# Attention taken two blocks of keys at a time: scores, values of two blocks, scores, then projection pieces

## The chip, the cores and the metric

The kernel runs on one core of one Trainium2 chip. The metric is device time in microseconds (us) of one execution, as the median of several. Engines that matter here are TensorE (PE in the profile, its weight loads PEld), VectorE (DVE), ScalarE (ACT), GpSimd (POOL) and SyncE (SP), which issues most DMAs. Each executes its own instruction stream in program order, and semaphores tie the streams together.

## What is computed

The input is 32 batches of 512 tokens by 512 features in float32, and a 512 x 512 adjacency matrix of zeros and ones. Two layers follow each other:

```
# layer 0
mi = x @ Wi.T ; mj = x @ Wj.T ; deg = adj.sum(1)
x  = layernorm(x + deg[:, None] * (mi + b) + adj @ mj)
# layer 1: 8 heads of 64
q, k, v = x @ Wq.T + bq, x @ Wk.T + bk, x @ Wv.T + bv
scores  = where(adj == 0, -inf, (q @ k.T) / 8)
x = layernorm(x + softmax(scores) @ v @ Wo.T + bo)
```

Everything is float32. The attention needs, per batch, 8 heads of 512 x 512 scores.

## The kernel before, in words

**Projections.** Each 512 x 512 product is made by a Strassen-like scheme of seven `piece` calls (line 420), numbered 1 to 7, on 256 x 256 quarters. One piece of kind `pj` (output projection), `v`, `q` or `k` is 8 matmul instructions with 256 moving columns; a piece of layer 0 (`l0`) has two terms and 16. A piece accumulates into a PSUM bank, and a reader then takes the bank's contents into SBUF: VectorE mostly (lines 454, 465, 474, 481), ScalarE for pieces 1 and 2 (lines 443, 463, 479). Pieces are grouped (line 408): 1 and 2 share a bank's contents, so do 6, 7 and 4, and 5 and 3. A later piece of a group adds on top of the earlier one, so its matmuls may start only once the reader of the earlier piece is done. There are two such banks, "mma" and "mmb" (line 86, one buffer each), and the kinds alternate between them. Between pieces stand `l0_gather` (line 316, matmuls with the adjacency matrix, read out by ScalarE at line 340), `l0_turn` (VectorE transpose, line 348, then a multiplication on GpSimd), `base` (two VectorE operations, line 354), `combos` (GpSimd, line 405: differences and sums of quarters), `stats` and `apply` (layer norm: VectorE lines 298 and 299, GpSimd 300 to 302, ScalarE 305), and `h_store`, `h_load`, `h_turn` (the layer-0 result goes to DRAM and comes back regrouped, and VectorE turns it, line 382).

**Attention.** A batch's attention has 8 steps (`STEPS`, line 549): two groups `g` of four heads, and four blocks `kc` of 128 keys for each. In a step, `scores(b, hp, kc)` (line 486) is called for two pairs of heads. It takes a PSUM tile "sc" (two buffers, line 93), makes 4 matmul instructions with 64 rows each, two at a time in the array, then ScalarE takes the exponential in place (line 494), and VectorE multiplies by the 0/1 edge matrix into an SBUF tile "e" (four buffers, lines 492 and 495). `values` (line 505) multiplies the "e" tiles of one block by V: 16 matmul instructions with 32 columns each, four at a time in the array. `presum` (line 497) adds up "e" tiles for the softmax denominators: on GpSimd for block 1 (line 501), on VectorE for blocks 2 and 3 (line 503). After a group's last block, `sums` (line 515) makes the denominators in another "sc" tile, `drain` (line 524) copies them, and `rest` (line 542) lists four reciprocals (`invert`, line 531), two multiplications (`scale`, line 540) and a reduction (`tell`, line 533).

**The order of the work** is written out by hand. `phase_a`, `phase_b` and `phase_c` (lines 567, 622, 644) list a batch's projection work, `by_steps` (line 686) cuts the list into 8 steps by estimated cost, and the loop from line 768 on emits each step. A step is: scores of this block for both pairs, values of the block before, then the pieces of that step. After each item with a cost, at most one waiting `presum` (the list `late`) and some of `rest` (the list `extra`) are emitted. While batch b attends, the loop projects batch b + 1 and finishes batch b - 1; the listing of the middle of the program for `PERIODS[n]` is, for steps 6 and 7: gather 0, k piece 5, turn 0, gather 1, k piece 3, turn 1, base 0, combos, gather 2, k piece 6, turn 2, base 1, gather 3, k piece 7, turn 3, combos, layer-0 piece 1, k piece 4. For steps 4 and 5 it begins with k piece 2, q piece 5, v piece 5, q piece 3, v piece 3.

Of the kernel before, what the change touches and what calls it, by code (L numbers as in the profile page):

```python
# [17 lines left out]
P = 128  # L18
# [7 lines left out]
def gnn_attention_kernel(  # L26
# [37 lines left out]
    B, N, D = x.shape  # L64
    NC = N // P
# [14 lines left out]
    def work(shape, name, bufs, dtype=FT):  # L80
        return pools.work.tile(shape, dtype, name=name, bufs=bufs)
# [7 lines left out]
    def ov_tile():  # L89
        return psum.tile([P, 512], FT, name="ov", bufs=2)  # L90

    def sc_tile():
        return psum.tile([P, 2, N], FT, name="sc", bufs=2)
# [147 lines left out]
    def ring_tile():  # L241
        return work([P, 2, Q], "ring", RING)
# [40 lines left out]
    def prefetch():  # L283
        while len(TILES) < min(len(KEYS), ring.used + RING) and KEYS[len(TILES)] in WS:
            t = ring_tile()
            nc.sync.dma_start(t, WS[KEYS[len(TILES)]])
            TILES.append(t)
# [105 lines left out]
    def ot_quarter(b):  # L393
        return lambda j, n: OT[b, j][:, :, Q * n:Q * n + Q]
# [86 lines left out]
                    nc.vector.scalar_tensor_tensor(d[:, c], pm[:, c, :], bc, p1[:, c, :], op0=OP.add, op1=OP.add)  # L481


    E, ES, PV, RL = {}, {}, {}, {}

    def scores(b, hp, kc):
        ps = sc_tile()
        for s in range(2):
            r = slice(s * HD, (s + 1) * HD)
            nc.tensor.matmul(ps[:, s, :], KT[b, hp // 2][r, hp % 2, kc * P:(kc + 1) * P],  # L490
                             QT[b, hp // 2][r, hp % 2, :], start=True, stop=True)
        e = E[hp % 2, kc] = work([P, 2, N], "e", 4)

        nc.scalar.activation(ps, ps, AF.Exp, scale=QSCALE)  # L494
        nc.vector.tensor_tensor(e, ps, edge[:, kc:kc + 1, :].to_broadcast([P, 2, N]), op=OP.mult)  # L495

    def presum(i, kc):
# [7 lines left out]
    def values(b, g, kc):  # L505

        if kc == 0:
            PV[g] = [ov_tile(), ov_tile()]
        for r in range(2):
            for h in range(4):  # L510
                c0 = (4 * g + h) * HD + 32 * r
                nc.tensor.matmul(PV[g][r][32 * h:32 * h + 32, :], V[b][:, kc, c0:c0 + 32], E[h // 2, kc][:, h % 2, :],  # L512
                                 start=(kc == 0), stop=(kc == NC - 1))

    def sums(g, kcs=(1,), last=1):

        if g not in RL:
            RL[g] = (sc_tile()[:, 0, :], work([P, N], "rl", 1))
        for kc in kcs:
            for h in range(4):  # L520
                src = ES[h // 2] if kc == 1 else E[h // 2, kc]
                nc.tensor.matmul(RL[g][0][32 * h:32 * h + 32, :], ones[:, :32], src[:, h % 2, :], start=(kc == 1), stop=(kc == last))  # L522

    def drain(b, g):

        j = 2 * (b * 2 + g)
        nc.scalar.activation(RL[g][1], RL[g][0], AF.Identity, accum_out=told[:, j:j + 1])
# [14 lines left out]
    def rest(b, g):  # L542
        return [(invert, g, c) for c in range(4)] + [(scale, b, g, 0), (scale, b, g, 1), (tell, b, g)]
# [5 lines left out]
    STEPS = 2 * HP  # L549
    PC, TR, GA = 1.73, 0.44, 1.9  # L550
    FLUSH = (0.0, None)

    def z(f, *a):
        return (0.0, f, *a)

    def pc(kind, b, i, bank):
        return (2 * PC if kind == "l0" else PC, piece, kind, b, i, bank)
# [5 lines left out]
    def banks(n):  # L563

        return ("a", "b") if n % 2 == 0 else ("b", "a")
# [21 lines left out]
    def first():  # L587


        g = [(TR + GA, l0_gather, 0, dc, "b") for dc in range(DC)]  # L590
        half = lambda name, i: z(combine, name, nc.gpsimd if name in ("wi", "wj") else nc.vector, i)
        y = [(8 * PC / 4, plain, ic) for ic in range(NC)]
        n = [(TR, l0_norm, 0, ic) for ic in range(NC)]
        return [g[0], z(graph_forms, 3), g[1], g[2], half("wv", 0), g[3], z(base, 0, 0), z(base, 0, 1), half("wv", 1),
                y[0], z(scaled, 0), half("wq", 0), half("wi", 0), y[1], z(scaled, 1), half("wq", 1), half("wi", 1), z(fold, 0), y[2], half("wk", 0), half("wj", 0),
                z(scaled, 2), n[0], y[3], half("wk", 1), half("wj", 1), n[1], (2 * PC, fold, 1), z(scaled, 3)]
# [16 lines left out]
    def project(m, i):  # L613

        res = [pc("pj", m, i, banks(m)[1])]
        if i == 1:
            res = [z(combos, TO, m, ot_quarter(m), (1,))] + res
        if i == 2:
            res = [FLUSH] + res + [z(combos, TO, m, ot_quarter(m), (2, 3, 4))]
        return res  # L620

    def phase_b(n):

        m = n - 2
        if m < 0:
            res = []
            side = [z(add_bo, 0, i) for i in range(2)]
            A, K = banks(n)
            for i, bank in ((2, A), (6, K), (5, A), (7, K), (4, K), (3, A)):
                res.append(pc("l0", n, i, bank))  # L630
                if i == 4:
                    res += [z(stats, n, 0)]
                if i in (2, 6):
                    res += [z(combine, "wo", nc.vector, int(i == 6))]
                res += side[:1]
                side = side[1:]
            return res + [z(apply, n, 0), z(stats, n, 1), (TR, l0_norm, n, 0), (TR, l0_norm, n, 1)]
        A = banks(n)[0]
        l0 = {i: pc("l0", n, i, A) for i in ORDER}
        return [l0[2], *project(m, 1), l0[6], *project(m, 2), l0[7], z(add_bo, n - 1, 0), *project(m, 6), l0[4], z(stats, n, 0),  # L640
                *project(m, 7), z(apply, n, 0), z(h_store, n, 0), l0[5], z(h_load, n, 0), z(add_bo, n - 1, 1), *project(m, 4),
                l0[3], z(stats, n, 1), z(h_turn, n, 0), *project(m, 5)]

    def phase_c(n):

# [53 lines left out]
    def last_steps():  # L699

        m = B - 2
        A, K = banks(B)
        p = {i: pc("pj", m, i, K if i in (6, 7, 4) else A) for i in ORDER}
        c = [z(combos, TO, m, ot_quarter(m), (1, 2)), z(combos, TO, m, ot_quarter(m), (3, 4))]
        own = [(4 * GA, last_part, c, 0) for c in range(2)]
        k = [pc("k", B - 1, i, K) for i in (7, 4)]
        return [[z(last_load), k[0], FLUSH, c[0], p[1], c[1], k[1]], [p[2], p[6]], [p[5], p[7], z(add_bo, B - 1, 0), z(add_bo, B - 1, 1)],
                [], [p[3], p[4]], [own[0], z(stats, m, 0), z(stats, m, 1)], [own[1], z(apply, m, 0), z(apply, m, 1), z(store, m)], []]

    def run(f):  # L710
        f[1](*f[2:])
# [36 lines left out]
    PERIODS = [first() + phase_c(0) + phase_a(1)]  # L748
    half = None
    for n in range(1, B):  # L750
        todo = phase_b(n) + phase_c(n) + phase_a(n + 1)
# [12 lines left out]
    for f in PERIODS[0]:  # L764
        run(f)
        if f[1] is combine:
            prefetch()
    for n in range(1, B + 1):
        b = n - 1
        extra = []  # L770
        for step in range(STEPS):
            g, kc = divmod(step, NC)
            scores(b, 2 * g, kc)
            scores(b, 2 * g + 1, kc)
            pb, pg, pk = (b, *divmod(step - 1, NC)) if step > 0 else (b - 1, 1, NC - 1)
            if pb >= 0:
                values(pb, pg, pk)
                if pk == NC - 1:
                    sums(pg, *(((1, 3), 3) if pb == B - 1 else ()))
                    drain(pb, pg)  # L780
                    extra = rest(pb, pg)
            late = [(presum, i, kc) for i in range(2) if kc > 0]
            if b == B - 1 and kc > 2 - g:

                late = []
            for f in PERIODS[n][step]:
                if f is FLUSH:
                    some = len(extra)
                else:
                    run(f)  # L790

                    some = 0 if f[0] == 0.0 else len(extra) if step == 0 else max(1, round(f[0] / PC))
                if some:
                    for g in late[:1] + extra[:some]:
                        g[0](*g[1:])
                    late, extra = late[1:], extra[some:]
            for g in late + extra:
                g[0](*g[1:])
            extra = []
    sums(1, (1, 2), 3)  # L800
    values(B - 1, 1, 3)
    sums(1, (3,), 3)
# [1 line left out]
    for ic in range(NC):  # L804
        c = slice(ic * P, (ic + 1) * P)
# [15 lines left out]
    with tc.If(flag > 0), tc.tile_pool(name="general", bufs=1) as pools.work:  # L821
# [30 lines left out]
        with tc.For_i(0, B, 1) as b:  # L852
            g = "general"
# [6 lines left out]
            for ic in range(NC):  # L860
                c = slice(ic * P, (ic + 1) * P)
# [10 lines left out]
            for ic in range(NC):  # L872
                c = slice(ic * P, (ic + 1) * P)
                nc.vector.tensor_copy(V[g][:, ic, :], product([(HT[g][:, dc, c], wv[:, dc, :]) for dc in range(DC)]))
            for hp in range(HP):
                c = slice(hp * P, (hp + 1) * P)
# [5 lines left out]
                for qb in range(NC):  # L882
                    ps = sc_tile()
# [28 lines left out]
            for ic in range(NC):  # L912
                c = slice(ic * P, (ic + 1) * P)
# [45 lines left out]
```

## Time and profile before

| what | value |
|---|---|
| median of 3 executions | 3689.72 us (3689.59 to 3689.89) |
| the profiled execution: its own time | 3689.89 us |
| its span | 3687.9 us |
| TensorE busy | 3662.2 us, 99% of the span |
| VectorE busy | 2393.1 us, 65% |
| GpSimd busy | 1939.0 us, 53% |
| ScalarE busy | 1029.4 us, 28% |
| DMA | 144 GB/s in the mean |

The span runs from the first to the last instruction in the profile; the execution's own time is 1.99 us more. Matmul ends are modelled in this profile and overlap, so the start times of neighbouring matmuls are the better measure of what each costs. Each engine's idle time is put down to what released it. Idle time of an engine that is not the bottleneck costs nothing.

### The profile page before, as it was taken

The numbers are of one execution on the slowest core, as the hardware profiler recorded it, in microseconds if no ns is written. First come the engines' busy times: TensorE is split into PE (matmuls) and PEld (weight loads), VectorE is DVE, ScalarE is ACT, GpSimd is POOL, SyncE is SP. The second block draws the span as 40 slices with busy tenths as digits, with TensorE's granted clock in tenths as the row PEclk, the third lists the DMA queues.
The fourth block names the chain that finished last, engine by engine and source line by source line (L and its number), as shares of the span: only waits on it lengthen the run. The fifth ranks groups of instructions, "written<-read, shape, count | busy, mean of one in ns | idle before, by whom it ended". The sixth has DMA issues, their size and how long they took to land.

```text
span 3687.9 us, 49638 instructions
## 1 busy us (share of the span) xinstructions
PE 3662.2 (99%) x18470; PEld 2511.0 (68%) x18470; DVE 2393.1 (65%) x3133; ACT 1029.4 (28%) x1485; POOL 1939.0 (53%) x1984
## 2 busy tenths in 40 slices
PE   9999999999999999999999999999999999999998
PEld 6766667666666666766666767666666676666663
DVE  4666666666666666666666666666666666666666
ACT  2232232222322223222223222232222322222322
POOL 3565545556455555455554555644555545555443
PEclk9999999999999999999999999999999999999999
DMA  8445455445555445554545544455544555455541
GB/s 257 141 120 143 137 155 160 135 133 138 149 160 148 132 132 149 151 163 122 140 138 154 160 138 131 137 149 159 149 131 132 148 152 161 125 140 138 154 135 50
DMA packets 797173, 530.02 MB, mean 144 GB/s; under 512 B 530432, under 2 KB 611840, under 8 KB 796928
## 3 DMA queue, kind: packets, MB, share of 16 engines
q1 hardware_dynamic: 780384, 494.78, 48.8%
q10 hardware_dynamic: 16320, 31.46, 2.3%
q8 instruction: 151, 2.47, 0.3%
q14 instruction: 94, 0.77, 0.1%
q0 software_dynamic: 224, 0.53, 0.0%
HBM read 453.25 MB, written 73.40 MB: 143 GB/s over the span
## 4 chain that ended last, share of the span: by engine, by line
PE 98%; DVE 1%; POOL 1%; ACT 0%; issue 0%; DMA 0%; SPq 0%; DVEq 0%; POOLq 0%; ACTq 0%
PE mma L436 31%; PE mmb L436 31%; PE sc L490 13%; PE ov L512 13%; PE mmb L334 4%; PE mma L334 3%; PE sc L522 2%; PE mmb L604 0%; PE mma L604 0%; POOL es L501 0%; DVE e L495 0%; DVE rl L531 0%; PE sc L730 0%; DMA big<-in_adj_dram 0%; POOL big L405 0%
## 5 line engine op out<-in xcount | busy, mean ns | idle before, releaser
L494 ACT ACTIVATE sc<-sc 128x1024 f32<-128x1024 f32 x512 | 493.1, 1007 | 1552.9 <-PE sc L490 1534.4
L495 DVE TENSOR_TENSOR e<-sc,edge 128x1024 f32<-128x1024 f32 x512 | 602.6, 1217 | 211.8 <-ACT sc L494 176.7
L436 PE MATMUL mmb<-ring,big 128*128 128x256 f32 x3144 | 731.5, 381 | 0.0
L436 PE MATMUL mma<-ring,big 128*128 128x256 f32 x3112 | 724.4, 381 | 1.5 <-DVE xh L454 0.8
L436 PEld LDWEIGHTS mmb<-ring,big 128*128 128x128 f32 x3144 | 592.1, 190 | 130.0 <-issue 26.8
L436 PEld LDWEIGHTS mma<-ring,big 128*128 128x128 f32 x3112 | 585.9, 190 | 132.3 <-issue 26.5
L490 PE MATMUL sc<-q,k 64*128 64x512 f32 x2048 | 510.5, 617 | 3.5 <-DVE e L495 3.5
L405 POOL TENSOR_TENSOR big<-big 128x512 f32<-128x512 f32 x376 | 492.2, 1336 | 27.0 <-ACT big L363 10.7
L512 PE MATMUL ov<-e,v 128*32 128x512 f32 x4096 | 492.6, 598 | 3.3 <-DVE oT L540 3.3
L501 POOL TENSOR_TENSOR es<-e 128x1024 f32<-128x1024 f32 x128 | 300.1, 2355 | 363.5 <-DVE e L495 363.5
L436 PE MATMUL mma<-big,ring 128*128 128x256 f32 x1808 | 430.5, 381 | 0.0
L436 PE MATMUL mmb<-big,ring 128*128 128x256 f32 x1776 | 422.8, 381 | 0.0
L300 POOL TENSOR_SCALAR mv<-mv 128x1 f32<-128x1 f32 x256 | 49.7, 194 | 664.6 <-DVE mv L299 652.2
L436 PEld LDWEIGHTS mma<-big,ring 128*128 128x128 f32 x1808 | 340.3, 190 | 74.6 <-issue 26.8
L436 PEld LDWEIGHTS mmb<-big,ring 128*128 128x128 f32 x1776 | 334.3, 190 | 72.9 <-issue 26.0
L512 PEld LDWEIGHTS ov<-e,v 128*32 128x32 f32 x4096 | 107.0, 109 | 351.5 <-issue 322.1
L204 POOL TENSOR_TENSOR xlo<-xh,xhi 128x512 fp32r<-128x512 f32 x128 | 162.6, 1281 | 338.7 <-ACT xhi L203 338.6
L490 PEld LDWEIGHTS sc<-q,k 64*128 64x128 f32 x2048 | 176.4, 186 | 211.3 <-issue 203.6
L349 POOL TENSOR_TENSOR big<-big,deg_r 128x512 f32<-128x512 f32 x124 | 173.2, 1397 | 263.7 <-DVE big L348 263.7
L503 DVE TENSOR_TENSOR es<-es,e 128x1024 f32<-128x1024 f32 x250 | 304.2, 1218 | 0.0
L454 DVE TENSOR_TENSOR xh<-xh,mma 128x512 f32<-128x512 f32 x186 | 126.7, 681 | 267.2 <-PE mma L436 267.2
L454 DVE TENSOR_TENSOR xh<-xh,mmb 128x512 f32<-128x512 f32 x186 | 126.7, 681 | 259.4 <-PE mmb L436 259.4
(157 smaller groups left out, 3658.8 us busy)
## 6 DMA issues: line engine op xcount, KB each, us to landing
ring<-wo SPq DMA_DIRECT2D x217, 256.0 KB, 2.8
ring<-wq SPq DMA_DIRECT2D x160, 256.0 KB, 3.7
ring<-wv SPq DMA_DIRECT2D x160, 256.0 KB, 3.3
ring<-wk SPq DMA_DIRECT2D x160, 256.0 KB, 3.2
ring<-wi SPq DMA_DIRECT2D x155, 256.0 KB, 2.6
ring<-wj SPq DMA_DIRECT2D x155, 256.0 KB, 2.6
xh<-in_x_dram SPq DMA_DIRECT2D x32, 1024.0 KB, 5.5
xa<-in_x_dram SPq DMA_DIRECT2D x124, 256.0 KB, 3.9
```

The costliest lines, as they stand in the source:

```text
L204: nc.gpsimd.tensor_sub(lo, xs, hi.bitcast(FT))
L334: nc.tensor.matmul(pm, parts[w][:, jc, :], adjR[:, jc, :], start=(w == 0 and jc == 0), stop=(w == 1 and jc == NC - 1))
L349: nc.gpsimd.tensor_tensor(XD[b][:, dc, :], XD[b][:, dc, :], deg_r, op=OP.mult)
L405: nc.gpsimd.tensor_tensor(dst, p, q, op=OP.subtract)
L436: nc.tensor.matmul(pm[:, c * Q:(c + 1) * Q], lhs, rhs, start=first, stop=(kc == 1 and n == len(terms) - 1), skip_group_check=True)
L454: nc.vector.tensor_tensor(d, d, pm, op=OP.add)
L490: nc.tensor.matmul(ps[:, s, :], KT[b, hp // 2][r, hp % 2, kc * P:(kc + 1) * P], QT[b, hp // 2][r, hp % 2, :], start=True, stop=True)
L494: nc.scalar.activation(ps, ps, AF.Exp, scale=QSCALE)
L495: nc.vector.tensor_tensor(e, ps, edge[:, kc:kc + 1, :].to_broadcast([P, 2, N]), op=OP.mult)
L501: nc.gpsimd.tensor_add(ES[i], E[i, 0], E[i, 1])
L503: nc.vector.tensor_add(ES[i], ES[i], E[i, kc])
L512: nc.tensor.matmul(PV[g][r][32 * h:32 * h + 32, :], V[b][:, kc, c0:c0 + 32], E[h // 2, kc][:, h % 2, :], start=(kc == 0), stop=(kc == NC - 1))
```

## The change

The loop now takes two blocks of keys at a time for batches 0 to 30 (`size = 2`); the last batch keeps single steps (`alone`). One double step is: scores of block kc for both pairs; values of the two blocks of the double step before; their masks; at a group's end sums and drain; scores of block kc + 1; then the pieces of both steps. `scores` no longer contains VectorE's multiplication, which becomes a function `mask` of its own, so that it can be placed in VectorE's stream. The masks of block kc come after the values; those of block kc + 1 go to the front of `late`. At a group's end the reciprocals and scalings are all emitted ahead of the pieces; otherwise the first mask of block kc + 1 is. `late` still gives up one entry after each item with a cost, is emptied ahead of `l0_norm` (whose transposes use "sc" tiles), and gives nothing after layer-0 piece 3.

In `phase_b`, `apply` and `h_store` of the first half move ahead of output-projection piece 7, `h_load` ahead of layer-0 piece 5, and `h_turn` ahead of layer-0 piece 3. In the last batch's list, output-projection piece 3 moves one step earlier.

```
-        return [..., z(stats, n, 0),
-                *project(m, 7), z(apply, n, 0), z(h_store, n, 0), l0[5], z(h_load, n, 0), z(add_bo, n - 1, 1), *project(m, 4),
-                l0[3], z(stats, n, 1), z(h_turn, n, 0), *project(m, 5)]
+                z(apply, n, 0), z(h_store, n, 0), *project(m, 7), z(h_load, n, 0), l0[5], z(add_bo, n - 1, 1), *project(m, 4),
+                z(h_turn, n, 0), l0[3], z(stats, n, 1), *project(m, 5)]
...
-                [], [p[3], p[4]], [own[0], ...
+                [p[3]], [p[4]], [own[0], ...
...
+    def mask(hp, kc):
+        ps = SC.pop(hp)
+        e = E[hp % 2, kc] = work([P, 2, N], "e", 4)
+        nc.vector.tensor_tensor(e, ps, edge[:, kc:kc + 1, :].to_broadcast([P, 2, N]), op=OP.mult)
...
+        alone = b == B - 1
+        size = 1 if alone else 2
+        for step in range(0, STEPS, size):
             g, kc = divmod(step, NC)
+            extra = []
+            for i in range(2):
+                scores(b, 2 * g + i, kc)
+            for f in due:
+                values(*f)
+            for i in range(2):
+                mask(2 * g + i, kc)
+            if due and due[-1][2] == NC - 1:
+                pb, pg = due[-1][:2]
+                sums(pg, *(((1, 3), 3) if pb == B - 1 else ()))
+                drain(pb, pg)
+                extra = rest(pb, pg)
+            due = [(b, g, kc + i) for i in range(size)]
+            late = [(presum, i, c) for _, _, c in due if c > 0 for i in range(2)]
...
+                for i in range(2):
+                    scores(b, 2 * g + i, kc + 1)
+                late = [(mask, 2 * g + i, kc + 1) for i in range(2)] + extra[-1:] + late
+                for f in extra[:-1] if extra else late[:1]:
+                    f[0](*f[1:])
+                late, extra = late[0 if extra else 1:], []
+            for f in [f for todo in PERIODS[n][step:step + size] for f in todo]:
...
+                    if f[1] is l0_norm:
+                        for g in late:
+                            g[0](*g[1:])
+                        late = []
                     run(f)
+                    some = 0 if f[0] == 0.0 else len(extra) if step == 0 and alone else max(1, round(f[0] / PC))
+                    if f[1] is piece and f[2] == "l0" and f[4] == 3:
+                        some = 0
                 if some:
                     for g in late[:1] + extra[:some]:
                         g[0](*g[1:])
                     late, extra = late[1:], extra[some:]
```

## The prediction

> **What bounds the kernel now.** I read the page first: busy shares and the chain that ended last.
>
> ```profile
> PE 3662.2 (99%) x18470; PEld 2511.0 (68%) x18470; DVE 2393.1 (65%) x3133; ACT 1029.4 (28%) x1485; POOL 1939.0 (53%) x1984
> PE 98%; DVE 1%; POOL 1%; ACT 0%; issue 0%; DMA 0%; SPq 0%; DVEq 0%; POOLq 0%; ACTq 0%
> ```
>
> TensorE is the chain. In the start times of single matmuls I find no hold-up worth naming from 150 to 3560 us: the kernel costs what its matmuls and its changes of matmul shape cost. So two questions decide: what fewer changes of shape give, and whether the new order makes TensorE wait. For the second I read the timeline of steps 6 and 7 of one batch; lines are start, length, engine, line, operation, and in brackets idle time and releaser.
>
> ```profile
> 1771.81 1.92 PE L512 MATMUL ov<-e,v 128*32 128x512 f32 x16
> 1773.67 1.21 PE L334 MATMUL mma<-adjR,xhi 128*128 128x512 f32 x4
> ...
> 1782.77 1.89 PE L436 MATMUL mmb<-big,ring 128*128 128x256 f32 x8
> 1784.59 1.99 PE L490 MATMUL sc<-q,k 64*128 64x512 f32 x8
> 1786.51 1.92 PE L512 MATMUL ov<-e,v 128*32 128x512 f32 x16
> 1788.36 1.21 PE L334 MATMUL mma<-adjR,xhi 128*128 128x512 f32 x4
> 1789.41 1.08 PE L334 MATMUL mma<-adjR,xlo 128*128 128x512 f32 x4
> 1790.32 1.89 PE L436 MATMUL mmb<-big,ring 128*128 128x256 f32 x8
> ```
>
> ```profile
> 1781.13 0.87 DVE L481 SCALAR_TENSOR_TENSOR k<-mmb,bk_c,p 128x256 f32<-128x256 f32 x2 [0.94 <-PE mmb L436]
> 1781.92 0.70 DVE L348 STREAM_TRANSPOSE big<-xa 128x512 f32<-128x512 f32 x1
> 1782.83 3.42 DVE L354 SCALAR_TENSOR_TENSOR xh<-b_r,deg_c,xh 128x512 f32<-128x512 f32 x2 [0.21 <-POOL xlo L204]
> 1786.17 0.68 DVE L474 TENSOR_TENSOR k<-mmb,k 128x512 f32<-128x512 f32 x1
> 1786.81 2.36 DVE L495 TENSOR_TENSOR e<-sc,edge 128x1024 f32<-128x1024 f32 x2
> ```
>
> The line to see is the fourth of these. K piece 6 starts at 1782.77 and could be read at +1.93 us (k pieces without a backlog: 1775.63 to 1777.56). VectorE, held by `base` for 3.42 us, reads it only at 1786.17, 1.5 us late. Nothing is lost, since scores and values (1784.59 to 1788.36) stand between it and piece 7 at 1790.32, which adds onto the same bank. This cover is what the change removes.
>
> **What the Trainium skill says.** "TensorEngine Tiling (Array Packing)", Key Properties: "Mode switching requires drain: Changing tiling mode (not just tile) drains the TensorE". The trace agrees and prices it, below. "TensorE: Matmul & The Clock Gate", its opening table, gives VectorE, ScalarE and GpSimd strict first-in first-out queues; in this trace VectorE's late read behind `base` is such a case. No page bears on this kernel's bank and tile reuse.
>
> **The gain, switch by switch.** Median distances of starts: pieces 216 ns, scores and values 429 ns per wave. Pieces to scores: 309 to the first wave and 533 to the second, so (309-216)+(533-429) = 197 ns. Scores to values: 526 and 454, so 97+25 = 122. Values to pieces: 542 and 320, so 113+104 = 217. Two old steps cost 2 x (197+122+217) = 1072 ns. A double step has pieces-scores 197, scores-values 122, values-scores (no clean case: 113 leaving values plus 104 entering scores = 217; between 0 and twice that if the pair behaves otherwise, which moves the total by 27 us either way), scores-pieces (one case, 526 and 320: 97+104 = 201): 737. Saved 335 ns, times 31 x 4 = 124 double steps: **-41.5 us**. Instruction counts on all engines and DMAs stay; `mask` is the same 1.22 us.
>
> **New waits.** Take t = 0 at a double step's first scores. Scores to values takes 1.92, two values blocks 3.57 (0.454+6x0.429+0.542), scores again 1.92; pieces start at 7.41, or 8.27 after a group's end (`sums`, 0.86). ScalarE starts exponentials 1.18 after each scores start, 1.0 each.
>
> *Masks and buffers.* The first masks need the "e" buffers of the block kc-2, free when the first values block ends: last wave 3.23 + 0.59, so masks run 3.9-5.1-6.2. The second scores need the "sc" tiles at 5.49 and 6.45: 0.3 and 0.2 us spare, hidden behind the values. Without cover this costs what VectorE is late.
>
> *Start of batch 0*: no values there, so the second scores wait for exp and mask: +1.6 us once.
>
> *Steps 0-1.* The reciprocals run from 7.2 (drain, as before 1.83 after `sums`) to 10.6, scalings to 11.9, the first layer-0 piece ends at 11.7: hidden. GpSimd gets `presum` ahead of the three output combos; combo 2 ends at about 21.6, its piece starts at 22.0: hidden by 0.4. With `add_bo` to 28.9, the layer-norm operations end at 31.4, and the two `apply` calls, now ahead of the next exponentials in ScalarE's queue, at 32.3, while those exponentials were due at 30.2. This eats the spare: 0.2 us.
>
> *Steps 2-3.* Moving `h_turn`: layer-0 piece 3 starts at p+5.2 (p = pieces' start), `h_turn` runs p+7.3-8.5, its data having landed at about t = 12.4 (`h_store` issue at 3.3, load issue 3.4 later, landing 5.7 after); SP's ring loads behind the earlier `h_load` are not needed till t = 11. Hidden. But old scores and values (3.8 us) no longer stand between piece 3 and v piece 1. `apply` of the second half ends 5.0 us after piece 3's add (1839.60, layer-norm operations to +4.2, apply 0.8): p+13.8, then the store's issue 0.37, then the copy of v piece 1, 0.58, ends p+14.8. V piece 2, on the same bank, was due at p+13.8: 0.9 us. With the 0.2: 1.1 x 30 batches = **+33 us** (0.2 to 1.5 each).
>
> *Steps 4-5.* Reciprocals and scalings (to 11.9) and one mask (13.0) come ahead of q piece 5's read (two at L481, 0.87), done at 13.9; q piece 3, same bank, is due at 13.4: 0.5 x 30 = **+15 us** (0 to 0.7).
>
> *Steps 6-7.* VectorE in order, starts from row pitches: masks to 6.2; mask three 7.7 (waits for its exponential at 7.7) to 8.9; mask four to 10.1; k piece 5 (starts 9.37) is read 11.3-12.1; `presum` to 13.2; turn to 13.9; `presum` to 15.0; k piece 3's read to 15.8; `presum` to 16.9; turn to 17.5; `base` 3.4 to 20.9 (with GpSimd working beside it, as at 1782.83); fourth `presum` 1.2 to 22.1; k piece 6's read to 22.7. K piece 6 starts at 9.37+2x3.57 = 16.5, gather 3 takes 1.86, and k piece 7, adding onto the same bank, is due at 20.1. TensorE waits **2.6-2.7 us**; behind it stand layer-0 piece 1, k piece 4 and the next scores, and none can pass. Bounds: `base` costs 0.71 each instead of 1.75 with GpSimd idle (both occur), giving 0.7; `presum` at the 1.7 that one row near the end has, giving 3.2. 29 batches (2 to 30): **+78 us**.
>
> *The last batch*: piece 3 of the output projection falls into a wait that exists (2.4 us ahead of 3630.5), but the next one is set by VectorE's reciprocals; at most 0.4 us, counted as none. Sum: -41.5+1.6+33+15+78 = **+86 us** on the span of 3687.9 (own time 3689.89, 0.17 above the median), so **3776 us** for the median.
>
> **Rivals.**
> *Faster.* VectorE keeps up: k piece 6 is read before 20.0 and the other waits vanish. For it: VectorE is only 65% busy and all spare times are near zero. Against: ahead of k piece 6 stand about 16.5 us of VectorE work between 3.9 and 18.4. It decides when the hold-ups per batch are below 41.5/30 = 1.4 us; with none, 3650.
> *Masks wait for both values blocks.* If the "e" buffers come free only at the second block's end, masks start at 5.6, and the second scores wait 1.4 and 0.2 us in every double step: 124 x 1.6 = 198 us; with the others about 3970, alone 3846. Nothing in the old trace shows it.
> *Balance.* Hold-ups at their low ends (0.7+0.5+0.2 per batch) give back just the gain: 3690, no change.
>
> **How the numbers follow.** Several waits with VectorE late: 0.75, own range 3705 to 3830 (low: 1.3 in steps 6-7, 0.5 and 0.2 in the others; high: 3.2, 1.5, 0.7 and the switches saving 20 less). Faster rival 0.15, balance 0.05, buffers 0.05. Low end 3682 takes in the balance; what is left out is the faster case and the buffers. 0.2% (7 us) is about what a measurement here can tell from no change.
>
> **What would show it.** After: 16 values waves become 32 instructions in a row between two scores; L436 on "mmb" or "mma" waiting for DVE k L474, 29 times, about 2.7 us; v piece 2 waiting for ACT's copy L443; q piece 3 for L481; VectorE's share of the chain up from 1% to some 4%. Wrong if TensorE's idle in the body stays under 40 us, or if the second scores wait for L495 in most double steps.

## The result and the profile after

The changed kernel takes 4074.6 us (median; 4073.5 to 4074.6), the one before 3689.65 in the same comparison: a ratio of 1.104 (95% interval 1.102 to 1.106). Slower was forecast, but 3776 with a range up to 3830: the size is far off. The profiled execution took 4074.61 us, its span is 4072.8, so 384.9 us more than the span before.

From the page of the changed kernel, the busy shares and the chain that ended last:

```profile
PE 3766.2 (92%) x18470; PEld 2591.9 (64%) x18470; DVE 2429.2 (60%) x3133; ACT 1047.2 (26%) x1485; POOL 2082.2 (51%) x1984
...
PE 73%; DVE 12%; POOL 8%; issue 4%; ACT 3%; ACTq 0%; DMA 0%; DVEq 0%; SPq 0%; POOLq 0%
```

The counts of instructions are those of before. TensorE has fallen from 98% to 73% of the chain; VectorE (forecast at some 4%) and GpSimd stand there with 20% together. GpSimd is busy 143 us longer with the same 1984 instructions. TensorE's own busy time has risen by 104 us, also with the same instructions: they ran at a lower clock in places.

TensorE's waits in the changed kernel (total us, times, longest us):

```profile
PE mma L436 <- DVE k L474: 67.5, 15, 4.5
PE mmb L436 <- DVE k L474: 66.3, 16, 4.5
PE mma L436 <- ACT p L443: 58.2, 15, 3.9
PE mmb L436 <- ACT p L443: 58.2, 15, 3.9
PE sc L490 <- DVE e L499: 23.5, 33, 1.5
...
PE mmb L436 <- DVE q L481: 3.4, 15, 0.2
```

These are the predicted places: k piece 7 behind VectorE's read of k piece 6, v piece 2 behind ScalarE's copy of v piece 1, q piece 3 behind VectorE's read of q piece 5 (its other half waits in "mma"). They come about as often as predicted. The first idles TensorE for 4.5 us in 29 places (once for 2.5) instead of 2.7, and the second for 3.9 instead of 0.9.

Timeline of steps 6 and 7 of one batch, whose double steps count from t = 0 at 1951.60; columns as in the prediction:

```profile
1967.37 1.56 DVE L507 TENSOR_TENSOR es<-es,e 128x1024 f32<-128x1024 f32 x1
1967.79 2.27 POOL L204 TENSOR_TENSOR xlo<-xh,xhi 128x512 fp32r<-128x512 f32 x1
1968.15 1.89 PE L436 MATMUL mmb<-big,ring 128*128 128x256 f32 x8
...
1970.10 3.44 DVE L354 SCALAR_TENSOR_TENSOR xh<-b_r,deg_c,xh 128x512 f32<-128x512 f32 x2 [0.54 <-POOL xlo L204]
...
1971.39 3.26 POOL L405 TENSOR_TENSOR big<-big 128x512 f32<-128x512 f32 x2
...
1973.46 2.28 DVE L507 TENSOR_TENSOR es<-es,e 128x1024 f32<-128x1024 f32 x1
1975.66 0.68 DVE L474 TENSOR_TENSOR k<-mmb,k 128x512 f32<-128x512 f32 x1
...
1976.39 3.03 PE L436 MATMUL mmb<-big,ring 128*128 128x256 f32 x8 [4.51 <-DVE k L474]
```

The order on VectorE is the predicted one. K piece 6 starts at t + 16.55 (16.5 predicted) and could be read some 1.9 us later, but `base` and a `presum` of 2.28 us stand ahead of the read. After the wait the 8 instructions of k piece 7 last 3.03 us; k piece 6 took 1.89. The windows of this stretch (length; busy us and instructions of TensorE, weight loads, VectorE, ScalarE, GpSimd; granted clock; DMA share; GB/s) say why:

```profile
1962.00:1976.00 14.00, 9.88 (x45) 7.99 (x43) 12.52 (x13) 2.59 (x5) 10.21 (x6) 1.00 0.22 57
1976.00:1990.00 14.00, 13.61 (x68) 8.81 (x72) 6.32 (x9) 2.51 (x3) 10.76 (x9) 0.88 0.27 76
```

Ahead of the wait's end the granted clock is 1.00, behind it 0.88. The trace's record of the clock shows the form of it: between 60 us and the last 100 us of the span there are 60 stretches at half clock, 40 of them 3.41 us long and 20 of them 6.83, together 273 us. Each of the 59 waits of 3.9 or 4.5 us has one: the 20 long stretches begin within the wait, the others 0.2 to 1.3 us after its end. The 60th, near 148 us, follows a wait of 1.8 us. In the kernel before there is none in this part. The prediction has no term for this.

Timeline of steps 2 and 3 of the same batch:

```profile
1908.49 0.26 POOL L302 TENSOR_SCALAR mv<-mv 128x1 f32<-128x1 f32 x1
1908.76 2.35 DVE L507 TENSOR_TENSOR es<-es,e 128x1024 f32<-128x1024 f32 x2
...
1908.83 1.20 POOL L300 TENSOR_SCALAR mv<-mv 128x1 f32<-128x1 f32 x1
...
1910.11 1.41 POOL L301 TENSOR_TENSOR mv<-mv,mhalf 128x1 f32<-128x1 f32 x1
...
1911.62 1.30 POOL L302 TENSOR_SCALAR mv<-mv 128x1 f32<-128x1 f32 x1
...
1912.96 0.81 ACT L305 ACTIVATE xh<-xh,mv 128x512 f32<-128x512 f32 x1 [3.36 <-POOL mv L302]
...
1914.21 0.58 ACT L443 COPY p<-mmb 128x512 f32<-128x512 f32 x1 [0.44 <-ACT xh L305]
...
1914.85 2.92 PE L436 MATMUL mmb<-ring,big 128*128 128x256 f32 x8 [3.86 <-ACT p L443]
```

Three layer-norm operations on one column, 128x1, took 1.20, 1.41 and 1.30 us on GpSimd while VectorE did `presum`. The last of them for the row before, at 1908.49, took 0.26; once VectorE had finished its sums, the three took 0.19, 0.55 and 0.26 (from 1913.78 on). So `apply` is about 3 us late, ScalarE's copy of v piece 1 waits behind it in the queue, and v piece 2 waits for the copy.

A second measure is taken from *start distances*: for each pair of neighbouring matmuls, the time from start to start less what such a pair takes without a wait. It includes what a slower clock adds. The sum over the body of the program is 437.1 us, against 9.9 in the kernel before:

| place | measured | predicted |
|---|---|---|
| k piece 7 (steps 6-7) | 138.0 (29 x 4.67, once 2.6) | 78 |
| v piece 2 (steps 2-3) | 121.3 (30 x 4.04) | 27 |
| second scores (steps 2-3) | 22.2 (30 x 0.74) | 6 |
| second wave of scores | 10.3 (64 x 0.16) | none |
| q piece 3 (steps 4-5) | 13.3 (32 x 0.41) | 15 |
| the rest, nearly all at half clock: 437.1 - 305.1 - 9.9 | about 122 | none |
| changes of shape (prediction's sum, not in the distances) | -41.5 | -41.5 |

427.2 more in distances less 41.5 is 385.7; the span grew by 384.9.

### The profile page after: what moved, and what is told of

It reads as the page before. It is cut to its first block, busy times and chain, and to the rows that moved or that the text cites. A ratio compares the mean times of both kernels' runs of the same rounds, so it can differ in the third digit from the quotient of the medians.

```text
span 4072.8 us, 49647 instructions
## 1 busy us (share of the span) xinstructions
PE 3766.2 (92%) x18470; PEld 2591.9 (64%) x18470; DVE 2429.2 (60%) x3133; ACT 1047.2 (26%) x1485; POOL 2082.2 (51%) x1984
## 4 chain that ended last, share of the span: by engine, by line
PE 73%; DVE 12%; POOL 8%; issue 4%; ACT 3%; ACTq 0%; DMA 0%; DVEq 0%; SPq 0%; POOLq 0%
PE mmb L436 24%; PE mma L436 24%; PE sc L490 11%; PE ov L516 10%; DVE rl L535 3%; POOL xlo L204 2%; DVE e L499 2%; DVE es L507 2%; POOL big L349 2%; PE sc L526 1%; DVE xh L354 1%; POOL mv L301 1%; PE mmb L334 1%; POOL mv L302 1%; DVE oT L544 1%
## 5 line engine op out<-in xcount | busy, mean ns | idle before, releaser
L436 PE MATMUL mma<-big,ring 128*128 128x256 f32 x1808 | 469.7, 406 | 71.4 <-DVE k L474 67.5
L436 PE MATMUL mmb<-big,ring 128*128 128x256 f32 x1776 | 459.2, 405 | 69.6 <-DVE k L474 66.3
L204 POOL TENSOR_TENSOR xlo<-xh,xhi 128x512 fp32r<-128x512 f32 x128 | 190.6, 1500 | 569.8 <-ACT xhi L203 569.8
L516 PE MATMUL ov<-e,v 128*32 128x512 f32 x4096 | 466.8, 595 | 2.9 <-DVE oT L544 2.9
L436 PEld LDWEIGHTS mma<-big,ring 128*128 128x128 f32 x1808 | 365.4, 204 | 154.0 <-DVE k L474 74.0
L305 ACT ACTIVATE xh<-xh,mv 128x512 f32<-128x512 f32 x252 | 197.6, 810 | 949.0 <-POOL mv L302 949.0
L300 POOL TENSOR_SCALAR mv<-mv 128x1 f32<-128x1 f32 x256 | 79.9, 312 | 521.2 <-DVE mv L299 508.8
L507 DVE TENSOR_TENSOR es<-es,e 128x1024 f32<-128x1024 f32 x250 | 344.3, 1388 | 0.0
L349 POOL TENSOR_TENSOR big<-big,deg_r 128x512 f32<-128x512 f32 x124 | 198.4, 1600 | 223.5 <-DVE big L348 214.7
L451 POOL TENSOR_TENSOR xh<-xh,p 128x512 f32<-128x512 f32 x186 | 231.2, 1272 | 143.7 <-ACT p L443 143.7
```

Source lines behind the costliest of these rows:

```text
L204: nc.gpsimd.tensor_sub(lo, xs, hi.bitcast(FT))
L305: nc.scalar.activation(y, y, AF.Identity, bias=mv[:, 4:5], scale=mv[:, 3:4])
L349: nc.gpsimd.tensor_tensor(XD[b][:, dc, :], XD[b][:, dc, :], deg_r, op=OP.mult)
L436: nc.tensor.matmul(pm[:, c * Q:(c + 1) * Q], lhs, rhs, start=first, stop=(kc == 1 and n == len(terms) - 1), skip_group_check=True)
L451: nc.gpsimd.tensor_tensor(d, d, p1, op=OP.add)
L507: nc.vector.tensor_add(ES[i], ES[i], E[i, kc])
```

## The theories and the experiments

My theory, A in all expectations: each long wait is a late reader at the place named; it is late because VectorE and GpSimd lengthen each other's work there; and TensorE, idle for some 4 us, gets half clock afterwards. The rivals, B and C as each expectation says: the low clock or the wait has another cause, or the wait only moves. For the kernels that mend the change, A is that the gain of 41.5 us is then left, B that new waits eat it. hold_6, copy_first, hold_2, fill_6 and combos_later were executed once each; four executions of the changed kernel lie within 1.2 us of each other. All edits are against the changed kernel, except that of `lists_only`.

**hold_6: no waiting `presum` is given out in steps 6-7 between gather 1 and k piece 7.**

```
+                    if step == 6 and (f[1] is l0_gather and f[3] > 0 or f[1] is piece and f[4] in (3, 6)):
+                        some = 0
```

> Changed kernel, but in steps 6 and 7 VectorE's presums are kept back until k piece 7 has been read: after gathers 1 to 3 and k pieces 3 and 6 nothing of the waiting list is emitted. Theory A (k piece 7 waits because VectorE reads k piece 6 late, and each such wait of over 4 us is followed by one or two stretches of 3.4 us at half the TensorE clock): the 30 waits of 4.6 us (138 us) fall under 0.5 us each, and the half-clock stretches that follow them go too, some 55 us; time 4074.6 - 138 - 55 = about 3880 us, and the number of half-clock stretches in the body falls from 60 windows to about 30. Theory B (the half clock has another cause, an average load, say): 4074.6 - 138 = about 3936 us. Theory C (GpSimd's lateness, not VectorE's, holds piece 7): no less than 4000 us.

3908.57 us. TensorE's waits in it:

```profile
PE mmb L436 <- ACT p L443: 58.1, 15, 3.9
...
PE mma L436 <- DVE k L474: 6.4, 15, 0.4
PE mmb L436 <- DVE k L474: 6.0, 14, 0.4
```

By start distances k piece 7 loses 17.3 us instead of 138.0; v piece 2 loses 121.1, as it did. Half-clock stretches fall from 60 to 30, from 273.1 to 136.5 us, and those left follow v piece 2's wait. The kernel before took 3687.39 beside this run (2.26 less than in the first comparison); allowing for this, 163.8 us are gained, 120.7 of them the wait itself. The other 43 go with the 30 stretches that are no longer there.

**copy_first: v piece 1, and so ScalarE's copy of it, comes ahead of `apply`.**

```
-            res = [z(apply, n, 1), z(h_store, n, 1), v[1], *project(m, 3), ...
+            res = [v[1], z(apply, n, 1), z(h_store, n, 1), *project(m, 3), ...
```

> Changed kernel, but with v piece 1 emitted ahead of the second half's apply and h_store, so that ScalarE copies v piece 1 before it waits for the layer norm. Theory A (v piece 2 waits for that copy, and the copy stands behind apply in ScalarE's queue): the 30 waits of 4.04 us (121 us) go, and their half-clock stretches (about 55 us); but apply, the store and the load come no earlier, so h_turn comes late by about 2.6 us for the masks at the next double step, and some 70 us of waits turn up at the second scores there: about 3970 us; without the new wait about 3900. Theory B (GpSimd's slow layer norm is what counts and any order leaves it): above 4040 us.

3966.18 us. V piece 2's wait is gone, k piece 7 keeps 137.9 us, and 31 half-clock stretches are left. The new wait isn't where I put it: it is at `sums`, 29.5 us in 31 places by start distances, and not at the second scores. In the waits of copy_first:

```profile
PE sc L526 <- DVE e L499: 23.7, 29, 1.9
```

A second one came too: `v` pieces wait for ScalarE's read at line 463, 13.1 us in 30 places by the waits. That the time is nearly the expected 3970 is chance: the new waits are some 43 us and not 70, and so the half clock gave back only about 28 us and not 55 (an estimate: 108.4 us gained, less 2.3 for the kernel before and 121.3 for the old wait, plus 42.6).

**hold_2: no waiting `presum` is given out behind output-projection piece 5 and v piece 1.** ScalarE's order stays; only what runs on VectorE beside the layer-norm operations is taken away.

```
+                    if step == 2 and f[1] is piece and (f[2], f[4]) in (("pj", 5), ("v", 1)):
+                        some = 0
```

> Changed kernel, but in steps 2 and 3 no presum is emitted after output-projection piece 5 and v piece 1, so VectorE runs none beside GpSimd's layer-norm operations. Theory A (GpSimd's three small operations took 1.20, 1.41 and 1.30 us instead of 0.19, 0.55 and 0.26 because VectorE's presums with two SBUF inputs ran at the same time): they take about 1.1 us in all again, apply ends some 3 us earlier, and v piece 2's wait falls from 4.04 to about 1 us, short enough for the clock to stay up: 4074.6 - 91 - 55 = about 3930 us. Theory B (they are slow for another reason): the wait stays at 4 us, and the time within 20 us of 4075.

3950.39 us. TensorE's waits in it:

```profile
PE mma L436 <- DVE k L474: 67.4, 15, 4.5
...
PE mmb L436 <- ACT p L443: 14.7, 15, 1.0
...
```

The other bank has as much again. V piece 2 loses 1.14 us a batch by start distances instead of 4.04: about the term of 0.9 that the prediction had for it, once GpSimd is undisturbed there. (The first of the three layer-norm operations took more than 1.1 us in 30 places of the changed kernel; here it never takes more than 0.54.) With copy_first this names both links, the copy's place behind `apply` and the two `presum` calls beside GpSimd. No half clock follows an idle time of 1.0 us: 30 stretches are left, at k piece 7. The time is 20 us above theory A's 3930, since the half clock gave back some 35 us and not 55.

**fill_6: 8 matmuls whose result nothing uses are put between gather 3 and k piece 7**, so that TensorE waits less long at a stretch. Reads and pieces are as in the changed kernel.

```
+    def fill(bank):
+        pm = mm_tile(bank)
+        for i in range(8):
+            nc.tensor.matmul(pm[:, 0:Q], ident, deg_r[:, 0:Q], start=True, stop=True)
...
-            res += g[i:i + 1] + k[i:i + 1] + [z(l0_turn, n, i)]
+            res += g[i:i + 1] + ([z(fill, A)] if i == 3 and n > 2 else []) + k[i:i + 1] + [z(l0_turn, n, i)]
```

> Changed kernel, with eight extra matmuls of 256 columns (3.4 us of TensorE work whose result is not used) in the wait between gather 3 and k piece 7, from batch 3 on. They write the bank that gather 3 was read out of, so TensorE idles less than 1.5 us at a stretch there. Theory A (half clock follows long idle): the half-clock stretches after k piece 7 go, those after v piece 2 stay: about 4074.6 - 55 = 4020 us, though 3.4 us of work per batch was added. Theory B (the slow matmuls after the waits have another cause): 4075 us or more.

4027.16 us: faster by 47 with more work on TensorE. The fill and k piece 7 in the timeline of one batch of fill_6 (line numbers are 5 higher behind the new function; a matmul of the fill leaves two records):

```profile
1952.25 3.72 PE L347 MATMUL mma<-deg_r,ident 128*128 128x256 f32 x16 [0.67 <-ACT big L340]
1956.07 1.99 PE L441 MATMUL mmb<-big,ring 128*128 128x256 f32 x8
```

K piece 7 takes 1.99 us here and 3.03 in the changed kernel. The half-clock stretches at it are gone, the 30 at v piece 2 remain. K piece 7 itself comes no earlier than it did (t + 24.77 in both kernels, in the median), so what is gained is the price of the low clock alone: 47.4 less 2.3 for the kernel before, 45 us over 29 places, 1.6 us each. It is a net price: the stretches at v piece 2 have grown from 102.4 to 153.6 us.

**combos_later: the first combos of steps 6-7 go from behind turn 1 to the end of the list**, so GpSimd does nothing beside the second `base` and the last `presum`. VectorE's instructions and their order stay.

```
-            if i == 1:
-                res += [z(combos, TX, n, xq, (1,)), z(combos, TA, n, aq, (1,))]
-        return res + [z(combos, TX, n, xq, (2,)), ...
+        return res + [z(combos, TX, n, xq, (1,)), z(combos, TA, n, aq, (1,)), z(combos, TX, n, xq, (2,)), ...
```

> Changed kernel, with GpSimd's first two combos of layer 0 moved from behind base 0 to behind turn 3, so that they no longer run beside VectorE's second base operation and last presum. VectorE's list is the same. Theory A (sharing between VectorE and GpSimd stretches both: that presum took 2.28 us instead of 1.22, base 1.75 instead of 0.71): k piece 6 is read about 2 us earlier, the wait of k piece 7 falls from 4.6 to about 2.6 us, and the clock stays up after it: 4074.6 - 60 - 55 = about 3960 us, or 4015 if some stretches of half clock stay. Theory B (only the number of VectorE operations ahead counts): within 10 us of 4075.

3969.26 us. TensorE's waits in combos_later, and VectorE's timeline in steps 6-7 of one batch:

```profile
PE mma L436 <- DVE k L474: 36.2, 15, 2.4
PE mmb L436 <- DVE k L474: 35.6, 16, 2.4
```

```profile
1921.68 2.42 DVE L354 SCALAR_TENSOR_TENSOR xh<-b_r,deg_c,xh 128x512 f32<-128x512 f32 x2 [0.55 <-POOL xlo L204]
1924.03 1.21 DVE L507 TENSOR_TENSOR es<-es,e 128x1024 f32<-128x1024 f32 x1
```

With GpSimd quiet the two `base` operations take 2.42 us instead of 3.44 and the `presum` 1.21 instead of 2.28. K piece 7 loses 76.4 us instead of 138.0, 2.55 each. So the lengthening comes from GpSimd's work beside it. That 2.55 is also near the 2.6 to 2.7 of the prediction is chance: `base` still begins 1.0 us later than forecast, and is 1.0 us shorter. An idle time of 2.4 us lies in between for the clock: 11 of 29 such waits have half clock.

**doubles_04: only steps 0-1 and 4-5 are doubled.**

```
-        size = 1 if alone else 2
-        for step in range(0, STEPS, size):
+        for step in range(STEPS):
+            if not alone and step % 2 and step - 1 in (0, 4):
+                continue
+            size = 2 if not alone and step in (0, 4) else 1
...
-            if alone:
-                if kc > 2 - g:
+            if size == 1:
+                if alone and kc > 2 - g:
```

> Changed kernel, but steps 2, 3, 6 and 7 are single again; only steps 0-1 and 4-5 are taken as double steps. Theory A (the waits belong to the two double steps left out): no wait over 1 us in the body and no half clock; 62 double steps save 335 ns each (20.8 us) and q piece 3's wait of 0.4 us (13 us) stays with some small ones (5 us): 3690 - 21 + 18 = about 3687 us, between 3672 and 3695. Theory B (double steps as such make the second scores wait): above 3700.

3686.98 us, ratio 0.9994 (0.9986 to 1.0003). Half the changes of shape are saved, 62 x 335 ns = 20.8 us. Start distances beyond the normal sum to 29.7 us, 12.3 of them at q piece 3, against 9.9 before: 19.8 more. The difference of -1.0 fits the measurement. There is no half clock.

**lists_only: the kernel before with the change's lists alone** (`apply`, `h_store` and `h_turn` earlier in `phase_b`, output-projection piece 3 earlier in the last batch). Single steps stay.

```
-                *project(m, 7), z(apply, n, 0), z(h_store, n, 0), l0[5], z(h_load, n, 0), z(add_bo, n - 1, 1), *project(m, 4),
-                l0[3], z(stats, n, 1), z(h_turn, n, 0), *project(m, 5)]
+                z(apply, n, 0), z(h_store, n, 0), *project(m, 7), z(h_load, n, 0), l0[5], z(add_bo, n - 1, 1), *project(m, 4),
+                z(h_turn, n, 0), l0[3], z(stats, n, 1), *project(m, 5)]
...
-                [], [p[3], p[4]], ...
+                [p[3]], [p[4]], ...
```

> The kernel before with the two lists of the change alone (phase_b's order and the last batch's piece 3 one step earlier), all steps single. Theory A (the waits come from the double steps): 3690 plus or minus 8 us. Theory B (the moved apply, load and turn make waits of their own, behind exponentials or the load's landing): 3700 to 3760.

3687.55 us, ratio 0.9996 (0.9987 to 1.0005). The moved lists cost nothing without the double steps; single scores and values between the pieces cover them.

**mend_base: all waits mended at once.** The edits of hold_6, hold_2 and copy_first, and

```
+                    if step == 4 and f[1] is piece and (f[2], f[4]) == ("k", 2):
+                        some = 0
...
-            if i in (1, 2):
-                res += [z(base, n, i - 1)]
+            if i in (2, 3):
+                res += [z(base, n, i - 2)]
...
-                z(apply, n, 0), z(h_store, n, 0), *project(m, 7), z(h_load, n, 0), l0[5], ...
+                *project(m, 7), z(apply, n, 0), z(h_store, n, 0), z(h_load, n, 0), l0[5], ...
...
+                while PERIODS[n][step][0][1] in (apply, h_store):
+                    run(PERIODS[n][step].pop(0))
                 for i in range(2):
                     scores(b, 2 * g + i, kc + 1)
```

> Changed kernel with all double steps, mended at each place where TensorE waited: presums held back in steps 6-7 until k piece 7 is read, and in steps 2-3 past the layer norm; base one place later, behind the next k piece's read; v piece 1 ahead of apply; no mask ahead of q piece 5's read; the first half's apply between the two rounds of exponentials. Theory A (all of the loss is these waits and the half clock behind them, and the switches do save 41.5 us): no wait over 1 us per place, no half clock in the body, 3690 - 41 + 15 = about 3660 us. Theory B (new waits take the place of the old ones, on late h_turn or late GpSimd sums): 3690 to 3800.

3702.56 us, ratio 1.0038 (1.0023 to 1.0052): slower than the kernel before by a little, so the rival was right. The old waits are gone and a new one stands at `sums`, 35.4 us in 57 places by start distances. One of them in the timeline of mend_base:

```profile
1757.32 1.25 DVE L382 STREAM_TRANSPOSE big<-xa 128x1024 f32<-128x1024 f32 x1 [4.36 <-DMA xa<-hd]
1758.49 2.31 DVE L499 TENSOR_TENSOR e<-sc,edge 128x1024 f32<-128x1024 f32 x2
...
1759.73 1.06 PE L526 MATMUL sc<-es,ones 128*32 128x512 f32 x8 [1.70 <-DVE e L499]
```

VectorE stands still for 4.36 us at `h_turn`, whose data hasn't landed, and the masks behind it, with `sums` waiting for their tiles, are late. VectorE's queue was held by a DMA. Of the waits 28 are of this kind, in steps 4-5, each about 2.5 us shorter than VectorE's idle time at `h_turn`, and together 17.9 us. Nearly all others are 0.44 us each and have no `h_turn` ahead. They fall in steps 0-1, where the held-back `presum` calls of steps 6-7 now run into the next double step and its masks start at t + 4.55.

**mend_more: the second `h_turn` behind q piece 2, the first ahead of the second scores, and turns 1, 2 and 3 together behind k piece 3.** The rest as in mend_base.

```
-            res += g[i:i + 1] + k[i:i + 1] + [z(l0_turn, n, i)]
+            res += g[i:i + 1] + k[i:i + 1] + [z(l0_turn, n, j) for j in ([0], [1, 2, 3], [], [])[i]]
...
-                   q[1], k[1], z(apply, m, 0), z(h_turn, n, 1), q[2], z(apply, m, 1), z(store, m),
+                   q[1], k[1], z(apply, m, 0), q[2], z(h_turn, n, 1), z(apply, m, 1), z(store, m),
...
+                while PERIODS[n][step][0][1] in (apply, h_store, h_turn):
...
+                    if step == 6 and (f[1] is l0_gather and f[3] > 1 or f[1] is piece and f[4] in (3, 6)):
```

> The mended kernel again, with the two waits that it had left (35 us ahead of the denominators' sums, behind late masks) taken on: h_turn of the second half goes behind the masks of step 4, so that they don't stand behind the landing of its load, and turns 1 to 3 and the presums of steps 6-7 move into VectorE's idle time ahead of k piece 6's and layer-0 piece 1's ends. Theory A (the 41.5 us of switches are there to be had once no wait is left): waits in the body under 15 us in all, no half clock, 3689 - 41 + 5 = about 3653 us. Theory B (the double step by itself leaves VectorE no room, and a wait comes up elsewhere): 3670 to 3700.

3660.33 us against 3689.35 of the kernel before beside it: ratio 0.9921 (0.9907 to 0.9934), faster than both kernels. The chain that ended last in mend_more, and TensorE's timeline in steps 6-7:

```profile
PE 97%; DVE 2%; POOL 1%; ACT 0%; issue 0%; DMA 0%; SPq 0%; DVEq 0%; POOLq 0%
```

```profile
1778.13 1.89 PE L436 MATMUL mmb<-big,ring 128*128 128x256 f32 x8
...
1781.70 1.89 PE L436 MATMUL mmb<-big,ring 128*128 128x256 f32 x8
```

K piece 7 starts 3.57 us after k piece 6, with no wait. VectorE no longer idles for the data of `h_turn`, and the masks of steps 0-1 start at t + 3.94. The edits were made together, so the run doesn't say what each is worth. Start distances beyond the normal sum to 22.0 us, 12.1 more than before; -41.5 + 12.1 is -29.4, and the span is 29.6 shorter than that of the profile before. So the predicted gain is real, and the change lost it in the order of VectorE's and GpSimd's work.

## Why the prediction was wrong, by its steps

**The gain, switch by switch: right.** Values to scores, which the old trace did not show, measured 542 ns to the first wave and 533 to the second, so 113 + 104 = 217 as taken; scores to pieces 526 and 320, 201 as taken. The balances of mend_more and doubles_04 close with 335 ns a double step.

**Steps 6-7: mechanism, place and number right, size wrong (78 predicted, 138.0 measured; above its high bound of 3.2).** The failing term is the length of `presum`, with a wait of `base` that was put at nothing. `presum` was taken at 1.2 us, and at most 1.7, from rows where GpSimd left it mostly alone. The third took 1.56 and the fourth 2.28. `base` began 1.0 us late (t + 18.5, not 17.5): 0.46 by the third `presum` and the turn behind it, 0.54 in waiting for GpSimd's `xlo`, itself 2.27 us long. (The line of `base` that the prediction shows has 0.21 us of this wait.) 1.0 for the late start and 1.0 from the start of the fourth `presum` to that of the read make the read end at t + 24.7 instead of 22.7, nearly the whole difference; `base` itself was as forecast. combos_later takes the neighbour away and gives 2.55 us; hold_6 takes the sums away and gives 0.59.

**Steps 2-3: the term for v piece 2 was 0.9 us with a high end of 1.5, and measured 4.04.** The failing term is "layer-norm operations to +4.2": durations of GpSimd in a trace where VectorE did no `presum` beside them. The double step puts `presum` calls at just this place, and the prediction did not ask what they would do to GpSimd. hold_2 shows the 1.1 us that are left without them.

For both, the Trainium skill has the mechanism, in "SBUF — State Buffer", section "SBUF: two separate sides": VectorE operations with two SBUF inputs and GpSimd operations that read SBUF share a pair of ports as "an exclusive lock, not a bandwidth split", and whichever starts first holds off the other for the whole instruction. The trace agrees in both directions: `presum` took 2.28 us instead of 1.21, and a GpSimd operation on one column 1.20 instead of 0.19, nearly one `presum` more. That it is the second SBUF input and not GpSimd's work as such shows in `mask`, which has the size of a `presum` but one of its inputs in PSUM: in the changed kernel its 120 operations that lay beside GpSimd work for over 90% of their length took 1.22 us in the median, as did the 335 without such a neighbour, and none of all 512 took more than 1.23. The prediction did use 1.75 for a `base` operation beside GpSimd, but only there.

**Half the TensorE clock: missing.** This is some 120 us of the 299 by which the forecast was low, and the prediction put it at nothing without a reason. The Trainium skill states the effect: "TensorE: Matmul & The Clock Gate", section "What's actually happening", has the clock go to half after an idle window of about 3.4 us, with a free-running window of 3413 ns; the section "Why this matters for your kernels" warns of TensorE gaps over about 3 us. The stretches of 3.41 and 6.83 us agree with that window. The idle time that it takes was shorter than the skill says: 2.4 us sufficed in 11 of 29 places of combos_later, and once in the trace before, at the very wait that the prediction names in the last batch:

```profile
3630.51 3.46 PE L490 MATMUL sc<-q,k 64*128 64x512 f32 x8 [2.42 <-DVE e L495]
```

These scores last 3.46 us instead of 1.99; the granted clock from 3630.9 to 3634.3 was 0.50. So with waits of 2.6 to 2.7 us forecast in 29 places, the clock belonged in the sum. Without it, the measured waits give 3689.7 - 41.5 + 305.1 = 3953, still outside the range. The two wrong sizes alone were enough: 60 us more at k piece 7 and 94 at v piece 2 make 3930 out of 3776.

How much of the 120 belongs to which wait stays open: the runs give 43 to 45 us for those behind VectorE (hold_6, fill_6), about 35 for those behind ScalarE (hold_2: 124.2 less 2.3 less 87.1 of wait), which is 80. The lengths of the remaining stretches change as well: those at v piece 2 last 3.4 us each in the mean in the changed kernel, 4.6 in hold_6 and 5.1 in fill_6. So removing one set of waits made the other set dearer, and the sum of the single prices falls short of the 120.

**The second scores: 0.2 predicted, 0.74 measured.** The step was right: `apply` and the store's issue stand ahead of the exponentials in ScalarE's queue. They ended at 1892.3 in one batch, while the exponential was due at 1889.7. The exponentials start 2.7 us late in all 30 batches, against 2.1 forecast (32.3 less 30.2). These 0.6 us are the error: 0.37 is the issue of the store, which the step left out, and the `apply` calls end 0.1 later than forecast.

**Steps 4-5 and batch 0: right.** Q piece 3 loses 0.41 us (0.5), batch 0's second scores 1.51 (1.6).

**Masks and buffers, and the rival of that name.** The masks start at t + 3.98 (3.9 predicted): "e" tiles come free with the first values block. The rival's 198 us did not come; its total near 3970 would have been closer than mine, for a wrong reason. **The faster rival** fell for this order, and is what mend_more comes near to (3650 with no hold-ups, 3660 measured). **Balance** fell as well; doubles_04, with half the double steps, is a case of it, with gain and waits equal. The sentence on what would make the prediction wrong named less idle time than 40 us; nothing in it looked above. (The low end of its own range, 3705, sums to 3708; nothing hangs on it.)

## What to carry to other kernels

When work is moved so that a VectorE operation with two SBUF inputs meets GpSimd work, price both at their length beside the other, down to the one-column operations on the GpSimd side; a trace in which they do not meet shows neither. A TensorE wait of 2 us or more can have a second price in the clock, so put it into the sum and the range. And before an item is held back or moved on an in-order queue, ask what it waits for: mend_base exchanged four waits for one at `sums`, half of it by letting VectorE stand still for a DMA.

## What was not expected of the hardware

- Half clock and length of the idle time: 1.0 us, none of 30 (hold_2); 2.4 us, 11 of 29 (combos_later); 3.9 us, 30 of 30 (each of the changed kernel, hold_6, fill_6) and 29 of 30 (combos_later); 4.5 us, 29 of 29 (each of the changed kernel, copy_first, hold_2).
- What separates these cases is where the idle time lies. Within a run, all half-clock stretches start on one grid with a pitch of 3.4133 us, to within 0.01 us. I laid this grid over the eleven traces, from 60 us after the start to 45 us before the end, and summed TensorE's idle time in each window. At full clock, all 211 windows with 2.0 us or more idle were followed by a window at half clock, 14 of the 30 with 1.79 to 1.99, and none of the 11471 with less. At half clock, all 95 windows with more than 0.6 us idle were followed by another at half clock, and all 225 with less by one at full clock. So 2.4 us cost nothing where the grid divided them, and 4.5 us could cost two windows.
- Filling a wait with unused matmuls made the kernel 45 us faster (fill_6), though it did not shorten the time until the piece behind it could start.
- Operations on one column on GpSimd, 0.19 to 0.55 us long alone, took 1.2 to 1.4 us each next to a row of VectorE sums, one after another: each was held off anew.
